# Gated window attention on one core: pairing each small query tile with part of a late one, and moving four kinds of work between steps and engines

## The chip, the cores and the metric

The kernel runs on one core of a Trainium2 chip. The metric is the device time of one execution in microseconds, given as the median of several runs. Everything is computed in float32 (one product is done in a float32 split into two passes, some small constants are bfloat16).

## The reference

Eight sequences of 1024 tokens with 512 features go through a layer norm, a masked attention with 16 heads of 32 features, and a gate computed from the same normalised input. Cut to what matters:

```python
xn = _layernorm(x)                       # x: (8, 1024, 512)
q, k, v = proj(Wq, bq), proj(Wk, bk), proj(Wv, bv)      # 16 heads, dk = 32
scores = einsum('bhid,bhjd->bhij', q, k) / sqrt(dk)
im = arange(L) % 256                     # four windows of 256 tokens
scores = where(im[:, None] >= im[None, :], scores, -1e30)
attn = einsum('bhij,bhjd->bhid', softmax(scores), v)
s = attn.reshape(B, L, D) @ Wo.T + bo
w = (weights >= 0) * 2 - 1
g = silu(clip((xn @ w.T) * scale + bias, -100, 100))
out = x + s * g
```

A token sees the tokens of all four windows whose place in their window is not later than its own. The kernel orders tokens by place first and window second, so that the mask becomes a causal one: in eight tiles of 128 tokens, query tile i sees key tiles 0 to i.

## The kernel before

**Groups and steps.** Four heads fill the 128 partitions, so a sequence has four head groups; a pair (b, g) is called a group, and there are 32. Every group takes nine steps, n = 0 to 8, in the main loop (L1257). A step holds attention work for the present group and, at the same time, for the next one (`nxt`), and it is filled up with projections, gate products and output products (`fill`, L1267).

**The quad.** Four PSUM banks form one tile, a *quad* (`quad`, L535), with 512 columns for each of four heads. There is one quad only, so every use waits until the readers of the use before have finished. A group uses it 16 times:

- Nine S quads (`maxima_quad`, L547) hold scores with queries on the partitions. `S_QUADS` says which query tile and which keys are in each. For the late query tiles 4 to 7, VectorE takes the maximum over the keys (L585, tile `pm`). For the early query tiles 0 to 3 VectorE takes the negated maximum (L579, `nm`), and ScalarE takes the exponentials straight from the quad (`own_probs`, L604, `pd`).
- Seven T quads (`probs_quad`, L747, in all steps but 0 and 3) hold the scores of late queries once more, with keys on the partitions and the maxima subtracted; ScalarE takes the exponentials of a quad in one instruction (L786, `p`). `attend_quad` (L792) multiplies them with the values one step later, and GpSimd adds them up for the row sums (`add_probs`, L814).

**Early tiles.** Their exponentials have to be turned, so that keys come onto the partitions. `own_turn` (L653) transposes blocks of 32x32 on VectorE (L658) into the tile `pt`, and 16 DMAs of one block each (`move`, L664), issued by SyncE, put the blocks into the tile `px`. There is one buffer for `pt` and one for `px`. `own_sums` (L614) makes the row sums on VectorE, and `own_attend` (L676) multiplies `px` with the values on TensorE. The moves are kept in a list, and every call of `fill` issues four of them. The tiles `pd` and `p` share two buffers.

`DIRECT` lists the S quads with early tiles and how many blocks of 128 keys these have: quad 0 (tile 3), quad 3 (tiles 2 and 0), quad 6 (tile 1, beside a part of tile 5). The turn and the sums of quads 0, 3 and 6 are done at the start of steps 1, 4 and 7, and the products of the turned blocks come three steps later: in steps 4 and 7, and in step 1 of the group after.

**Filling work.** Two further PSUM banks (`bank`, L123) take the products that fill the steps. Such a product (`product`, L383) has four chunks with a planned cost of 0.86 each; after the last one the bank is emptied: values, queries and keys by ScalarE (L421, L438), gate and output products by VectorE (two instructions each, L470 and L471, L866 and L867). A product can't start in a bank that has not been emptied. The order of filling work in each group is written in `STEADY`, `OPENING` and `CLOSING` (L932): V values, q, k queries and keys, G and H gate products, O and P output products, N the next sequence's layer norm; what stands before "|" may be taken a group early. How much of it goes into a step is planned by `share`: an even part of the remaining cost, less a fixed number for each step (L1153), with a least amount after an S quad (L1329) and a wanted amount between a T quad and its S quad (`gap`, L1309).

**Other steps' work.** In step 0 ScalarE copies the attention result of the group before (`copy_heads`) and its row sums (`sum_keys`, L832). VectorE inverts those sums in four parts, two in step 3 and two in step 5 (`invert`, L836), and applies them in step 6 (L840).

Each engine runs its instructions in the order in which they are written.

Of the kernel before, what the change touches and what calls it, by code (L numbers as in the profile page):

```python
# [46 lines left out]
    [(2, 0, 384), (0, 0, 128)],  # L47
    [(4, 0, 512)],
    [(5, 0, 512)],
    [(1, 0, 256), (5, 512, 768)],  # L50
    [(7, 512, 1024)],
    [(6, 512, 896), (4, 512, 640)],
# [17 lines left out]
DIRECT = {0: 4, 3: 4, 6: 2}  # L70

@with_exitstack
def tile_gated_window_attention(
# [307 lines left out]
    vt, qt, kt, gd = {}, {}, {}, {}  # L381

# [34 lines left out]
    def values_work(b, it):  # L417
        def after(ps):

            vt[b, it] = vpool.tile([P, D], F32, tag="v", name=f"v_{b}_{it}")  # L420
            nc.scalar.copy(vt[b, it], ps)  # L421
# [9 lines left out]
    def heads_work(b, g, half, which):  # L431
# [3 lines left out]
        def after(ps):  # L435
            if (b, g) not in into:
                into[b, g] = qk.tile([P, L], F32, tag=which, name=f"{which}_{b}_{g}")
            nc.scalar.activation(  # L438
                into[b, g][:, half * HALF : (half + 1) * HALF], ps, AF.Identity,
                bias=bias[:, g : g + 1], scale=SCALE if which == "q" else 1.0,  # L440
            )
# [172 lines left out]
    def own_sums(b, g, n):  # L614
        it = direct[b, g, n]
        if n == 0:
# [3 lines left out]
        for i, lo, hi, at in it["own"]:  # L620
            part = view[:, :, :, at // P : (at + hi - lo) // P]
            nc.vector.tensor_reduce(  # L622
                inverse[b, g][:, i, :], part.rearrange("p h r k t -> p h r (k t)"), AX.XY, ALU.add
            )
        if n == 6:
            nc.vector.reciprocal(inverse[b, g], inverse[b, g])
# [26 lines left out]
    def own_turn(b, g, n):  # L653
        it = direct[b, g, n]
        size = NH * DIRECT[n] * P
        t = swapped.tile([P, NH * HALF], F32, tag="pt", name=f"pt_{b}_{g}_{n}")
# [4 lines left out]
        def move(q, r):  # L661
            if "x" not in it:
                it["x"] = swapped.tile([P, NH * HALF], F32, tag="px", name=f"px_{b}_{g}_{n}")
# [4 lines left out]

        moves.extend(lambda q=q, r=r: move(q, r) for r in range(NH) for q in range(NH))
# [6 lines left out]
    def own_attend(b, g, n):  # L676
        it = direct.pop((b, g, n))
        k = DIRECT[n]
# [18 lines left out]
        if n == 6:  # L697
            copy_heads(b, g, 0)

    def copy_heads(b, g, f):  # L700
        aT[b, g, f] = heads.tile([P, HALF], F32, tag=f"a{f}", name=f"aT_{b}_{g}_{f}")
        nc.scalar.copy(aT[b, g, f], av[b, g, f])
# [117 lines left out]
    def sum_keys(b, g):  # L820
# [11 lines left out]
        nc.scalar.copy(sums[b, g], ps)  # L832
# [75 lines left out]
    def row_work():  # L908
# [24 lines left out]
        "V4 G3 V5 q20 | V7 G4 V6 k20 q21 G5 k21",  # L933
        "O0 O1 O2 | q30 N0 k30 O3 q31 G6 k31 G7",
        "N1 O4 O5 | O6 k00' V0' q00' O7 V1' q01'",
        "V2' V3' | k01' q11' G0' k10' G1' k11' q10' G2'",
# [4 lines left out]
        "N1 G6 G7 V1' V2' k00' q00' V3' q01'",  # L941
        "k01' G0' | q11' k10' R G1' k11' q10' G2'",
# [4 lines left out]
        "H3 O4 H4 O5 H5 O6 H6 O7 |",  # L947
# [203 lines left out]
    def side(b, g):  # L1151
        if (b, g) not in sides:
            sides[b, g] = Beside(beside(b, g), [1.8, 1.43, 2.7, 0.86, 1.86, 1.86, 1.36, 2.3, 1.86])  # L1153
# [78 lines left out]
    start += values_work(0, 0) + values_work(0, 1) + values_work(0, 2) + values_work(0, 3)  # L1232
    start += heads_work(0, 0, 1, "k")
    start += woven(heads_work(0, 1, 0, "k"), fw_turns[:2])
# [3 lines left out]
    for n in range(NQ):  # L1238
        if n in (1, 4, 7):
            own_turn(0, 0, n - 1)  # L1240
            own_sums(0, 0, n - 1)
        maxima_quad(0, 0, n)
        if n == NQ - 1:
# [5 lines left out]
        if n in (5, 8):  # L1249
            own_attend(0, 0, n - 5)  # L1250
        if n not in (4, 7):
            move_some(9)
        start.fill(share)
    start.fill(1e9)

    steps = [(b, g, n) for b in range(B) for g in range(NC) for n in range(NQ)]
    for s, (b, g, n) in enumerate(steps):  # L1257
# [20 lines left out]
        if nxt and n in (1, 4, 7):  # L1278
            own_turn(*nxt, n - 1)
            own_sums(*nxt, n - 1)  # L1280
        spent = 0.0
        if n in (0, 3):
# [4 lines left out]
            if before:  # L1287
                attend_quad(*before)
            if nxt:
                own_probs(*nxt, n)  # L1290
            if n == 0 and old:
                copy_heads(*old, 1)
                spent += fill(1.2, turns=0)
                sum_keys(*old)
                spread_inverse(b, g)
            elif n == 0:
                spread_inverse(b, g)
        else:
# [3 lines left out]
            if n == 1:  # L1302
                own_attend(b, g, 6)
# [119 lines left out]
```

## Time and profile before

| what | value |
|---|---|
| median of 3 runs | 2381.21 us (2376.27 to 2389.77) |
| the profiled execution, its own time | 2391.47 us |
| its span, first to last instruction | 2389.7 us |
| TensorE (PE) busy | 2131.2 us, 89% |
| VectorE (DVE) busy | 1516.1 us, 63% |
| GpSimd (POOL) busy | 1141.7 us, 48% |
| ScalarE (ACT) busy | 946.0 us, 40% |
| mean granted TensorE clock | 0.969 |
| DMA, 16 engines | 28.9% busy on the queue that SyncE issues to |

Busy time counts every instruction of an engine from its start to its end, overlaps once. A matmul's end is modelled, so PE's busy time is not PE at its peak. The waits list names, for each engine and line, the idle time before an instruction and the instruction whose semaphore ended it. In the profile an fp32 matmul shows as two instructions. "PE t L753" is the first matmul of a T quad, "PE s L555" and "PE s L565" are the first of an S quad.

### The profile page before, as it was taken

What the parts mean: (1) busy time and instruction counts of PE and PEld (TensorE: products, weight loads), DVE (VectorE), ACT (ScalarE), POOL (GpSimd) and SP (SyncE); (2) the same over time, 40 slices, a digit from 0 to 9 for tenths busy, and PEclk for the clock granted to TensorE, in tenths of its full rate; (3) what the DMA queues carried; (4) which work ended last, traced back from release to release, by engine and by line L of the source; (5) the groups of instructions that cost most, each with busy time, mean ns of one, the idle gap of its engine ahead of it and who ended that gap; (6) DMA issues with size and microseconds to landing.
All of it is one profiled execution on the core that took longest, in us unless ns stands there. A gap on an engine that the chain in (4) does not pass through costs nothing. (4 is left out here: it accounts for less than half of the span.)

```text
span 2389.7 us, 59945 instructions
## 1 busy us (share of the span) xinstructions
PE 2131.2 (89%) x25775; PEld 897.8 (38%) x25775; DVE 1516.1 (63%) x1667; ACT 946.0 (40%) x1312; POOL 1141.7 (48%) x1037
## 2 busy tenths in 40 slices
PE   8899899999989898998989989898889888899877
PEld 4334333333333333333334333333333333333332
DVE  4657666766666656676566765667656667576763
ACT  3245444444443343344433343434434344443331
POOL 1056454554635445363454544555445555445556
PEclk9999999999999999999999999999999999999989
DMA  6222223332223322243212332223312233223233
GB/s 199 62 61 73 68 52 82 98 114 55 69 72 102 102 60 53 72 115 94 68 50 78 105 98 63 59 78 100 107 50 74 78 101 100 51 59 89 81 89 103
DMA packets 136610, 196.12 MB, mean 82 GB/s; under 512 B 31116, under 2 KB 51864, under 8 KB 136344
## 3 DMA queue, kind: packets, MB, share of 16 engines
q1 hardware_dynamic: 135640, 191.10, 28.9%
q8 instruction: 203, 3.33, 0.6%
q10 hardware_dynamic: 704, 1.18, 0.1%
q14 instruction: 63, 0.52, 0.1%
HBM read 72.62 MB, written 35.65 MB: 45 GB/s over the span
## 5 line engine op out<-in xcount | busy, mean ns | idle before, releaser
L814 POOL TENSOR_TENSOR p<-p,p 128x512 f32<-128x512 f32 (+1 forms) x736 | 890.6, 1241 | 484.9 <-ACT p L786 481.9
L585 DVE TENSOR_REDUCE pm<-s 128x4 f32<-128x2048 f32 (+3 forms) x256 | 480.2, 1886 | 345.3 <-PE s L565 343.9
L786 ACT ACTIVATE p<-t 128x2048 f32<-128x2048 f32 (+1 forms) x224 | 393.7, 1758 | 562.6 <-PE t L763 279.2
L604 ACT ACTIVATE pd<-s,nm 128x384 f32<-128x384 f32 (+3 forms) x512 | 224.4, 535 | 353.7 <-DVE nm L579 232.3
L565 PE MATMUL s<-k,q 32*128 32x512 f32 (+3 forms) x3072 | 318.4, 507 | 15.0 <-ACT p L786 10.5
L395 PE MATMUL v_ps<-wvT,xnT 128*32 128x512 f32 (+3 forms) x2792 | 254.2, 489 | 16.6 <-ACT sums L832 10.2
L395 PE MATMUL k_ps<-xnT,wk 128*32 128x512 f32 (+3 forms) x2632 | 254.5, 505 | 3.3 <-ACT sums L832 2.0
L579 DVE TENSOR_REDUCE nm<-s 128x2 f32<-128x1024 f32 (+3 forms) x256 | 195.8, 817 | 91.5 <-PE s L565 90.8
L395 PE MATMUL q_ps<-xnT,wq 128*32 128x512 f32 (+3 forms) x2672 | 247.9, 488 | 6.3 <-ACT xnT L366 4.1
L395 PE MATMUL o_ps<-woT,aT 128*32 128x512 f32 (+3 forms) x2624 | 244.4, 497 | 8.6 <-DVE s L867 6.9
L658 DVE STREAM_TRANSPOSE pt<-pd 128x2048 f32<-128x2048 f32 (+1 forms) x96 | 187.5, 1953 | 86.1 <-ACT pd L604 68.7
L763 PE MATMUL t<-q,k 32*128 32x512 f32 (+3 forms) x2048 | 232.5, 536 | 0.0
L799 PE MATMUL av<-p,v 128*32 128x512 f32 (+3 forms) x2048 | 230.2, 534 | 0.1
L868 POOL TENSOR_TENSOR s<-s,xb 128x512 f32<-128x512 f32 x63 | 84.4, 1340 | 220.1 <-DVE s L867 188.0
L472 POOL TENSOR_SCALAR y<-y 128x512 f32<-128x512 f32 x64 | 41.9, 655 | 308.0 <-DVE y L471 245.3
L622 DVE TENSOR_REDUCE ls<-pd 128x4 f32<-128x2048 f32 (+3 forms) x128 | 183.2, 1451 | 0.0
L493 PE MATMUL y_ps<-fwT,x 128*128 128x512 f32 x472 | 148.7, 451 | 35.5 <-ACT q L438 14.9
L565 PEld LDWEIGHTS s<-k,q 32*128 32x128 f32 x3072 | 129.3, 185 | 101.4 <-ACT p L786 72.2
L753 PE MATMUL t<-shift,neg 3*128 3x512 bf16 (+3 forms) x1024 | 88.8, 356 | 74.7 <-ACT pd L604 38.9
L395 PEld LDWEIGHTS v_ps<-wvT,xnT 128*32 128x32 f32 x2792 | 84.3, 111 | 167.4 <-issue 128.1
L466 POOL TENSOR_TENSOR x<-xnT,x 128x512 fp32r<-128x512 f32 x59 | 75.9, 1286 | 143.2 <-ACT x L465 141.8
L395 PEld LDWEIGHTS o_ps<-woT,aT 128*32 128x32 f32 x2624 | 81.9, 110 | 159.5 <-issue 139.9
(111 smaller groups left out, 1938.4 us busy)
## 6 DMA issues: line engine op xcount, KB each, us to landing
px<-pt SPq DMA_DIRECT2D x1024, 64.0 KB, 2.0
px<-pt SPq DMA_DIRECT2D x512, 32.0 KB, 1.9
g<-t SPq DMA_DIRECT2D x64, 256.0 KB, 2.0
gb<-g SPq DMA_DIRECT2D x64, 256.0 KB, 3.1
xb<-in_L_attn_x_dram SPq DMA_DIRECT2D x64, 256.0 KB, 3.3
out_dram<-s SPq DMA_DIRECT2D x63, 256.0 KB, 2.5
x<-in_L_attn_x_dram SPq DMA_DIRECT2D x62, 256.0 KB, 3.5
wk<-wk_d SPq DMA_DIRECT2D x31, 256.0 KB, 3.3
```

The lines of the kernel that those rows point to most:

```text
L395: nc.tensor.matmul(hold[0][cols, lo:hi], lhsT=lhsT[:, cols], rhs=rhs[:, lo:hi], start=(i == 0 and lo == 0), stop=(i == n - 1), skip_group_ ...
L493: nc.tensor.matmul(hold[0], lhsT=part[i][:, c, :], rhs=wT["fw"][:, c, :], start=(i == 0 and c == 0), stop=(i == 1 and c == NC - 1),)
L565: nc.tensor.matmul(sc[:, h, at : at + hi - lo], lhsT=qt[b, g][head_rows(h), i * P : (i + 1) * P], rhs=kt[b, g][head_rows(h), lo:hi], start ...
L579: nc.vector.tensor_reduce(nm[:, k, h : h + 2], sc[:, h : h + 2, at : at + hi - lo], AX.X, ALU.max, negate=True,)
L585: nc.vector.tensor_reduce(pm[:, 0 if lo == 0 else 1, i - 4, :], sc[:, :, at : at + hi - lo], AX.X, ALU.max,)
L604: nc.scalar.activation(view[:, h, at // P : (at + hi - lo) // P], it["sc"][:, h, at : at + hi - lo].rearrange("p (k r t) -> p k r t", r=NH ...
L622: nc.vector.tensor_reduce(inverse[b, g][:, i, :], part.rearrange("p h r k t -> p h r (k t)"), AX.XY, ALU.add)
L658: nc.vector.transpose(t[:, 0:size], it["p"][:, 0:size])
L763: nc.tensor.matmul(sc[:, h, at : at + w], lhsT=kt[b, g][head_rows(h), j * P : (j + 1) * P], rhs=qt[b, g][head_rows(h), HALF + lo : HALF + ...
L786: nc.scalar.activation(pt[:, :, :width], sc[:, :, :width], AF.Exp, scale=1.0)
L799: nc.tensor.matmul(av[b, g, 1][head_rows(h), lo : lo + w], lhsT=vt[b, j][:, g * P + h * DK : g * P + (h + 1) * DK], rhs=pts[b, g, n][:, h, ...
L814: nc.gpsimd.tensor_tensor(t[:, hs, lo : lo + w], t[:, hs, lo : lo + w], p[:, hs, at : at + w], ALU.add)
```

## The change

The S quads are put together anew. Tile 2 (384 keys) shares quad 3 with 128 keys of tile 4; tile 1 (256 keys) moves from quad 6 to quad 5, with the same part of tile 5; tile 0 (128 keys) moves from quad 3 to quad 7, with 384 keys of tile 6; quad 8 is now a part of tile 7 alone. All quads keep 512 columns. `DIRECT` now has four quads: 0, 3, 5 and 7, with 4, 3, 2 and 1 blocks of 128 keys, in place of 4, 4 and 2.

There are thus four turns a group, each with 16 moves. Those of quads 0, 5 and 7 stand at the start of steps 1, 6 and 8; that of quad 3 stands within step 3, after some filling work. The sums of quad 0 are split: two heads before, two heads after the S quad of step 1. The products of the turned blocks stand in step 3 (quad 0), 6 (quad 3), 8 (quad 5) and in step 1 of the group after (quad 7). The turned tile of quad 7 lies in a buffer of the pool for temporaries in place of `pt`.

In step 0, VectorE empties the banks of values, queries and keys; it also makes the copy of the attention result and the copy of the row sums, which ScalarE made before. The four inversions stand in steps 2, 4, 6 and 7, and are applied in step 8. One gate product and one key projection change places between the lists of the groups, and the planned amounts of filling work are new. The first group's order is adapted (not shown).

```diff
-    [(2, 0, 384), (0, 0, 128)],
+    [(2, 0, 384), (4, 512, 640)],
     [(4, 0, 512)],
+    [(1, 0, 256), (5, 512, 768)],
     [(5, 0, 512)],
-    [(1, 0, 256), (5, 512, 768)],
+    [(0, 0, 128), (6, 512, 896)],
     [(7, 512, 1024)],
-    [(6, 512, 896), (4, 512, 640)],
...
-DIRECT = {0: 4, 3: 4, 6: 2}
+DIRECT = {0: 4, 3: 3, 5: 2, 7: 1}
...
-            nc.scalar.copy(vt[b, it], ps)
+            if by_vector[0]:
+                nc.vector.tensor_copy(vt[b, it], ps)
+            else:
+                nc.scalar.copy(vt[b, it], ps)
...
+            if by_vector[0]:
+                nc.vector.tensor_scalar(dst, ps, factor, bias[:, g : g + 1], ALU.mult, ALU.add)
...
+        small_one = n == 7 and b < B - 1
+        if small_one:
+            t = temp(f"pt_{b}_{g}_{n}")
...
+        while it["left"]:
+            move_some(1)
...
-        nc.scalar.copy(sums[b, g], ps)
+        nc.vector.tensor_copy(sums[b, g], ps)
...
-        "V4 G3 V5 q20 | V7 G4 V6 k20 q21 G5 k21",
+        "V4 V5 q20 | V7 G4 V6 k20 q21 G5 k21",
         "O0 O1 O2 | q30 N0 k30 O3 q31 G6 k31 G7",
-        "N1 O4 O5 | O6 k00' V0' q00' O7 V1' q01'",
-        "V2' V3' | k01' q11' G0' k10' G1' k11' q10' G2'",
+        "N1 O4 O5 | O6 k00' V0' q00' O7 V1' q01' k01'",
+        "V2' V3' | q11' G0' k10' G1' k11' q10' G2' G3'",
...
-            sides[b, g] = Beside(beside(b, g), [1.8, 1.43, 2.7, 0.86, 1.86, 1.86, 1.36, 2.3, 1.86])
+            sides[b, g] = Beside(beside(b, g), [1.9, 1.17, 2.7, 1.72, 0.95, 1.81, 2.0, 1.4, 2.2])
...
-        if nxt and n in (1, 4, 7):
-            own_turn(*nxt, n - 1)
-            own_sums(*nxt, n - 1)
+        if nxt and n in (1, 6, 8):
+            done = {1: 0, 6: 5, 8: 7}[n]
+            own_turn(*nxt, done)
+            own_sums(*nxt, done, slice(0, 2) if n == 1 else slice(0, NH))
         spent = 0.0
+        by_vector[0] = n == 0
...
+            if n == 3 and nxt:
+                own_attend(*nxt, 0)
...
             if n == 1:
-                own_attend(b, g, 6)
+                own_attend(b, g, 7)
...
-            elif n in (4, 7) and nxt:
-                own_attend(*nxt, n - 4)
+            elif n in (6, 8) and nxt:
+                own_attend(*nxt, n - 3)
             if nxt:
-                gap = {1: 1.6, 2: 0.4, 4: 1.2, 6: 0.2, 7: 0.8}.get(n, 1.2)
+                gap = {1: 2.0, 2: 0.5, 4: 2.2, 6: 0.2, 7: 1.8, 8: 1.0}.get(n, 1.4)
...
+                if n == 1:
+                    own_sums(*nxt, 0, slice(2, NH))
...
-        if old and n in (3, 5):
-            invert(*old, n - 3)
-            invert(*old, n - 2)
-        if old and n == 6:
+        if old and n in (2, 4, 6, 7):
+            invert(*old, {2: 0, 4: 1, 6: 2, 7: 3}[n])
+        if old and n == 8:
             normalise_heads(*old)
...
-            want = max(want, 2.45 if len(S_QUADS[n]) > 1 else 2.35)
+            want = max(want, {5: 2.9, 7: 2.8}.get(n, 2.35))
...
-            fill(max(want, (2.4 if n == 0 else 4.4) - spent) if nxt else want)
+            if n == 3 and nxt:
+                want -= fill(1.6)
+                own_turn(*nxt, 3)
+                own_sums(*nxt, 3)
+            fill(max(want, 2.4 - spent) if nxt else want)
```

## The prediction

> **What bounds the kernel now.** I read the page first, then one windows answer for each step number, then PE's waits, and last the timeline of one group.
>
> ```profile
> span 2389.7 us, 59945 instructions
> ...
> PE 2131.2 (89%) x25775; PEld 897.8 (38%) x25775; DVE 1516.1 (63%) x1667; ACT 946.0 (40%) x1312; POOL 1141.7 (48%) x1037
> ```
>
> TensorE (PE) is the bound, with 258.5 us idle. The change leaves its instructions alone: nine S quads of 512 columns, 40 blocks of turned products and the same filling work. So the time can only move with PE's idle time. The windows run from a step's first quad matmul to the next step's, for steps 0 to 8 in this order; each sum is over 27 groups, the second to the 28th.
>
> ```profile
> sum 232.15, PE 186.97 PEld 63.38 DVE 177.24 ACT 123.53 POOL 93.93; mean PE 6.92 PEld 2.35 DVE 6.56 ACT 4.58 POOL 3.48
> sum 219.18, PE 196.56 PEld 73.72 DVE 171.79 ACT 83.20 POOL 35.92; mean PE 7.28 PEld 2.73 DVE 6.36 ACT 3.08 POOL 1.33
> sum 204.95, PE 202.22 PEld 82.15 DVE 94.94 ACT 80.03 POOL 106.28; mean PE 7.49 PEld 3.04 DVE 3.52 ACT 2.96 POOL 3.94
> sum 235.13, PE 195.22 PEld 89.09 DVE 135.26 ACT 100.61 POOL 71.05; mean PE 7.23 PEld 3.30 DVE 5.01 ACT 3.73 POOL 2.63
> sum 213.30, PE 196.37 PEld 82.63 DVE 191.31 ACT 104.01 POOL 132.67; mean PE 7.27 PEld 3.06 DVE 7.09 ACT 3.85 POOL 4.91
> sum 193.85, PE 193.40 PEld 67.27 DVE 87.83 ACT 68.05 POOL 132.25; mean PE 7.16 PEld 2.49 DVE 3.25 ACT 2.52 POOL 4.90
> sum 210.21, PE 176.10 PEld 81.02 DVE 158.17 ACT 86.30 POOL 126.03; mean PE 6.52 PEld 3.00 DVE 5.86 ACT 3.20 POOL 4.67
> sum 247.51, PE 217.01 PEld 114.38 DVE 150.31 ACT 90.23 POOL 116.73; mean PE 8.04 PEld 4.24 DVE 5.57 ACT 3.34 POOL 4.32
> sum 198.80, PE 197.45 PEld 88.03 DVE 98.20 ACT 69.19 POOL 147.14; mean PE 7.31 PEld 3.26 DVE 3.64 ACT 2.56 POOL 5.45
> ```
>
> Sum less PE, over 27, is the idle time a group: 1.67, 0.84, 0.10, 1.48, 0.63, 0.02, 1.26, 1.13 and 0.05 us in steps 0 to 8, 7.18 in all, of 72.4. PE's waits say on what:
>
> ```profile
> PE t L753 <- ACT pd L604: 38.9, 33, 4.2
> PE s L555 <- ACT p L786: 33.9, 31, 2.8
> PE t L753 <- DVE pm L585: 32.8, 22, 3.9
> PE y_ps L493 <- ACT q L438: 14.9, 8, 2.9
> PE y_ps L493 <- ACT v L421: 13.7, 5, 2.7
> ...
> PE v_ps L395 <- ACT sums L832: 10.2, 5, 2.0
> ```
>
> The first three are the quad: about once a group in step 6 (pd), step 7 (p), steps 1 and 4 (pm). The others are banks not yet emptied, in steps 3 and 0. The timeline shows step 6 and the queue of SyncE (SP):
>
> ```profile
> 1209.96 7.47 SPq L664 DMA_DIRECT2D px<-pt  x12
> ...
> 1224.29 0.33 SPq L482 DMA_DIRECT2D g<-t  x1
> 1224.66 12.37 SPq L664 DMA_DIRECT2D px<-pt  x12
> 1224.98 1.29 DVE L579 TENSOR_REDUCE nm<-s 128x2 f32<-128x512 f32 x2 [0.72 <-PE s L565]
> 1226.19 1.21 DVE L585 TENSOR_REDUCE pm<-s 128x4 f32<-128x1024 f32 x1
> 1227.52 1.57 ACT L604 ACTIVATE pd<-s,nm 128x256 f32<-128x256 f32 x4 [3.87 <-DVE pm L585]
> 1229.13 0.40 PE L753 MATMUL t<-shift,neg 3*128 3x384 bf16 x8 [1.51 <-ACT pd L604]
> ```
>
> In a quad shared by an early and a late tile, ScalarE starts pd only after pm, though it needs only nm. A move takes 0.63 us of SP (7.47 / 12), and one g write held the moves behind it by some 6.8 us.
>
> **The change, step by step.** Idle us a group, before to after.
>
> *Step 6 to steps 5 and 7.* Quad 6 becomes plain, so step 6's wait for pd goes. Quad 5 gets the old quad 6's readers: its S quad begins at 1223.75, the next T quad 5.38 later; the quad itself takes 1.16, and PE filled 2.7 for a planned 2.45. Now 2.9 is planned, some 3.2 us: wait 1.0. Quad 7 reads 2 x 0.413 (nm) + 1.755 (pm, the row of 1536) + pd, 4 x 0.385 less the overlap of the 256 row (1.57 of 1.90): 3.85 in place of 4.07. With 2.8 planned: wait 0.9. Both could be 0.4 to 1.5.
>
> *Step 7's wait for p.* Here p takes the buffer that pd left, so it waits for the turn and sums (ACT p waited 66.0 us for L622). That pair is now in steps 6 and 8. Step 6: turn 1.24, sums 1.18, then p of 256 columns, 1.03: 3.5 after pd, while PE has T quad 0.8, products 1.06 + 0.80 (12 of 16 blocks' 1.06) and 0.2: wait 0.65. Step 8: turn about 0.7 (rows 2.31 and 1.24 halved on), sums 0.67, no longer than the T quad's own 1.4: nothing new, 0.05. Step 7: no such wait left beyond the 0.9.
>
> *Steps 1 and 4, pm behind turn and sums.* In step 1 1.12 of the 2.24 sums goes behind pm. In step 4, turn and sums were 2.31 + 1.71 + 0.67 = 4.69; now they begin within step 3 and take about 1.75 + 1.71 = 3.46, and PE needs pm only some 4.8 after the T quad starts. 0.63 to 0.2. In step 1 VectorE also has step 0's new copies ahead of it, so I take 0.84 to only 0.5 (0.1 to 1.5).
>
> *Step 3's banks.* Bank copies stand on ScalarE behind pd: eight instructions, 4 x 0.594 + 4 x 0.385 = 3.92, now four, 2.38; nm and pm are 2.58 against 2.73. Banks come free 1.7 sooner, about the wait itself: 1.48 to 0.4 (0 to 1.5).
>
> *Step 0.* The result copy (0.59) and sums copy (0.62) stood on ScalarE behind nm (2.43) and pd (2.42); on VectorE they wait for nm alone. That ends the waits on ACT sums. But the waits there on DVE s and y (o_ps, v_ps, sum, mT: about 28 us in all) stay, and the result copy is put ahead of those empties. With 0.34 less filling planned: 1.67 to 1.0 (0.3 to 1.7). VectorE takes 0.69 for a bank (rows L470, L866) where ScalarE takes 0.59 to 0.62: two copies, and at 3.4 of filling against 3.44 a product, with three products in four of them V, q or k, under one bank: about 1.9 us a group. The Trainium skill ("VectorE: DVE Perf Modes", Specifications) says VectorE sits closer to SBUF and ScalarE closer to PSUM, which speaks against this move. The rows agree in sign, by 0.1 us an instruction; going by distance alone the step would lose 0.3 us instead of gaining, and I go by the queue, since 4.85 us of queue stood ahead on ScalarE.
>
> *Inversions* (4 x 0.92) move behind pm, into steps 2, 6 and 7, whose VectorE is 3.5 to 5.9 busy of 7.6 to 9.2 us, and step 4, which loses turn work: nothing. Step 8's apply (0.84) stands where 3.64 was busy: nothing; were it before pm, 0.84. Quad 7's turned tile holds one of five temporary buffers for some 13 us; all waits for such a buffer now are 2.5 us (ACT t on a write to out_dram), so nothing, and up to 0.7 where gate and output banks had to wait for one. The gate product that leaves group 0 takes with it 8.4 of the 28 us of step 0 at most; this is within that step's 1.0.
>
> The sum: 1.0, 0.5, 0.1, 0.4, 0.2, 1.0, 0.65, 0.9, 0.05 = 4.8; gain 2.38.
>
> *SP and px.* Moves go from 48 to 64 a group, 10.1 us more of SP; smaller blocks issue no faster (32 KB and 64 KB both about 0.59). px has one buffer. For quad 7 it comes free 3.0 into step 8 and is needed 1.46 into step 1: 7.36 - 3.0 + 7.6 + 1.46 = 13.4 us. Sixteen moves take 10.1, landing 2.0, two other issues 1.2: 13.3. No slack, where before there were three steps and PE waited for px once (2.6 us). Held moves as shown would take 17.1 + 2.0 = 19.1: wait 5.7. SP's own waits list has 106 such holds (g 51, out_dram 55; 443 us), 0.37 a step, 4.2 us each. Over the 1.5 steps in which moves remain that is 0.55 a group, each costing about 2 after what SP can catch up: 1.1. Quad 0, with 1.6 of slack, and the others I take at zero. Bounds 0 to 4.
>
> Net 2.38 - 1.1 = 1.28 a group, 35 us over 27 groups; the opening and the other five groups I leave even (10 either way). Against the profiled execution, 2391.47 (span 2389.7 and 1.8 outside), that is 2357; it stands 10.3 above the median, so the median becomes 2347.
>
> **Rivals.** No wait for px (SP runs ahead, holds fall elsewhere): 2.38 x 31 = 74, so 2307; with steps 0 and 3 at their low ends 2280. For: before, one wait in 31 groups. Against: the slack is gone.
>
> No change: VectorE is full in steps 0 and 1. It is busy 12.9 of 16.7 there; with 1.9 more it has 14.8 of about 15.1, in order, and each late pm holds the next T quad. If step 1 idles at 1.6 and step 0 keeps 1.2, the net is zero: 2380. For: DVE's st waits up to 4.8 us for a load of x. Against: VectorE waits for pd in step 0 anyway, so the copies fit there.
>
> Slower: the px chain. If moves are held in most groups, PE waits at the turned products of step 1 (and 3); a mean of 3.4 us a group costs 1.0 net, 31 us: 2412. It decides from 2.4 us a group on. For: 19.1 against 13.4. Against: holds come in a third of the steps.
>
> That VectorE empties next to nothing in step 0 is possible too; the two copies are the part that counts.
>
> **How the numbers follow.** The forecast (2318 to 2369) 0.44, no px wait 0.20, VectorE full 0.17, px chain 0.19. About 0.5%, 12 us, is what a measurement of this kernel can tell from no change. Faster 0.64, same 0.17, slower 0.19. The range 2293 to 2405 leaves out the low part of the second case and the high half of the last. The forecast's own range is 2318 to 2369.
>
> **What would show it.** Right: no "t <- pd" in step 6 but two in steps 5 and 7, near 1 us each; "s <- p" in step 6 at half its size; "v_ps <- ACT sums" gone; "av <- px" some 30 us. Wrong: idle in steps 0 and 1 of 2.5 or more together; "av <- px" under 5 or over 75 us; PE busy other than 2131 by over 15.

## The result and the profile after

The changed kernel takes 2456.72 us (median of 4 runs, 2454.36 to 2462.35), the kernel before 2381.93 beside it: a ratio of 1.0315, 95% interval 1.028 to 1.035. It is slower by 75 us. The forecast was 2347, and the time lies above the whole range. Of the rivals the px chain came nearest, with 2412.

First the page of the changed kernel, its span and TensorE's busy time.

```profile
span 2452.6 us, 60762 instructions
...
PE 2145.0 (87%) x25655; PEld 895.5 (37%) x25655; DVE 1574.2 (64%) x1802; ACT 911.0 (37%) x1241; POOL 1139.7 (46%) x1038
```

The profiled execution took 2454.36. Its span is 62.9 us longer than the one of before: 13.8 of it is TensorE's busy time (2145.0 against 2131.2, though the profile has 120 matmuls fewer), 49 its idle time (307.6 against 258.5).

Now the windows, cut as before at the first matmul of each step's quad, steps 0 to 8 in this order, sums over the 27 groups from the second to the 28th.

```profile
sum 199.57, PE 186.90 PEld 63.58 DVE 167.53 ACT 91.26 POOL 74.32; mean PE 6.92 PEld 2.35 DVE 6.20 ACT 3.38 POOL 2.75
sum 207.31, PE 198.65 PEld 73.61 DVE 164.52 ACT 97.75 POOL 29.00; mean PE 7.36 PEld 2.73 DVE 6.09 ACT 3.62 POOL 1.07
sum 205.80, PE 201.04 PEld 84.92 DVE 127.08 ACT 79.72 POOL 102.39; mean PE 7.45 PEld 3.15 DVE 4.71 ACT 2.95 POOL 3.79
sum 200.87, PE 200.02 PEld 103.42 DVE 141.12 ACT 89.97 POOL 61.12; mean PE 7.41 PEld 3.83 DVE 5.23 ACT 3.33 POOL 2.26
sum 209.01, PE 199.00 PEld 74.60 DVE 144.16 ACT 86.21 POOL 120.16; mean PE 7.37 PEld 2.76 DVE 5.34 ACT 3.19 POOL 4.45
sum 251.61, PE 216.28 PEld 98.53 DVE 149.90 ACT 115.06 POOL 189.31; mean PE 8.01 PEld 3.65 DVE 5.55 ACT 4.26 POOL 7.01
sum 208.24, PE 181.39 PEld 74.36 DVE 154.00 ACT 49.20 POOL 89.21; mean PE 6.72 PEld 2.75 DVE 5.70 ACT 1.82 POOL 3.30
sum 233.43, PE 204.94 PEld 89.69 DVE 139.46 ACT 91.33 POOL 121.51; mean PE 7.59 PEld 3.32 DVE 5.17 ACT 3.38 POOL 4.50
sum 265.98, PE 175.50 PEld 74.56 DVE 129.81 ACT 76.92 POOL 175.59; mean PE 6.50 PEld 2.76 DVE 4.81 ACT 2.85 POOL 6.50
```

Sum less PE, over 27, beside the prediction's numbers, in us a group:

| step | 0 | 1 | 2 | 3 | 4 | 5 | 6 | 7 | 8 | all |
|---|---|---|---|---|---|---|---|---|---|---|
| before | 1.67 | 0.84 | 0.10 | 1.48 | 0.63 | 0.02 | 1.26 | 1.13 | 0.05 | 7.18 |
| predicted, without px | 1.0 | 0.5 | 0.1 | 0.4 | 0.2 | 1.0 | 0.65 | 0.9 | 0.05 | 4.8 |
| after | 0.47 | 0.32 | 0.18 | 0.03 | 0.37 | 1.31 | 0.99 | 1.06 | 3.35 | 8.08 |

Steps 0 to 7 come to 4.73 where 4.75 was predicted. That the sums agree so well is partly luck: steps 0 to 3 idle 1.0 us less than predicted, steps 4 to 7 about 1.0 more. What made the kernel slower within these groups stands in step 8. PE's waits name it:

```profile
PE av L709 <- DMA px<-pt: 71.5, 25, 5.5
PE t L776 <- ACT pd L612: 70.3, 64, 4.2
PE s L563 <- DVE pm L593: 44.3, 29, 2.6
```

In the profile before, the first and the third of these were small (the second was 38.9):

```profile
PE s L555 <- DVE pm L585: 6.8, 9, 2.7
...
PE av L686 <- DMA px<-pt: 2.6, 1, 2.6
```

In step 8 of the 27 groups the first row has 47.8 us in 12 waits and the third 37.3 in 20: 85.1 of the 90.5 us of idle time there. The rows of single groups in the windows answer for step 8 (columns: length, then busy time of PE and its matmuls, of the other engines, granted clock, DMA) show which groups; these are the four of the second sequence:

```profile
456.39:469.86 13.47, 6.14 (x69) 2.72 (x68) 5.21 (x7) 1.88 (x1) 10.57 (x13) 0.87 0.23 70
534.73:541.76 7.03, 4.45 (x68) 2.12 (x68) 5.12 (x7) 2.35 (x2) 4.29 (x4) 1.00 0.42 131
604.99:612.43 7.44, 7.41 (x100) 2.97 (x100) 3.83 (x5) 3.50 (x4) 5.29 (x5) 1.00 0.08 17
674.56:687.45 12.89, 8.88 (x101) 3.27 (x100) 5.06 (x7) 3.34 (x4) 7.03 (x7) 0.87 0.41 124
```

Two causes are visible. The first and second groups have 68 matmuls (the same step of before had 85 to 113): the quads and the attention products, and as filling only eight matmuls of one output product. And the first and fourth groups are 5 to 6 us longer than the others, at a lower clock. The timeline of a first group shows why (steps 6 to 8, SyncE's queue, its releasers on GpSimd and what waits):

```profile
1323.29 4.96 SPq L684 DMA_DIRECT2D px<-pt  x8
...
1331.86 0.64 SPq L892 DMA_DIRECT2D out_dram<-s  x1
1332.60 0.54 SPq L490 DMA_DIRECT2D g<-t  x1
...
1334.47 2.45 SPq L684 DMA_DIRECT2D px<-pt  x4
1336.73 1.27 POOL L891 TENSOR_TENSOR s<-s,xb 128x512 f32<-128x512 f32 x1 [4.89 <-DMA xb<-in_L_attn_x_dram]
1338.02 0.64 SPq L892 DMA_DIRECT2D out_dram<-s  x1
...
1339.40 8.20 SPq L684 DMA_DIRECT2D px<-pt  x8
1343.48 0.64 PE L709 MATMUL av<-px,v 128*32 128x128 f32 x16 [4.34 <-DMA px<-pt]
...
1349.49 0.24 PE L563 MATMUL s<-after,place_of 32*128 32x128 bf16 x4 [2.42 <-DVE pm L593]
```

Quad 5's sixteen moves go out as 8, 4 and 4 (the row x8 at 1339.40 begins with the last four; quad 7's follow). After the first eight the queue stands 3.6 us, until 1331.86, before a write to out_dram. The last four stand behind a second such write, which waits for GpSimd's `s`, which waits for a load of xb. They are issued from 1339.40 on; four times some 0.62 and a landing of 2.0 give 1343.9, and PE's products begin at 1343.48. Then the next S quad waits 2.42 us for pm, with nothing to fill in.

### The profile page after: what moved, and what is told of

Read it like the earlier page. It is cut to its first block, busy times and chain, and to the rows that moved or that the text cites. A ratio compares the mean times of both kernels' runs of the same rounds, so it can differ in the third digit from the quotient of the medians.

```text
span 2452.6 us, 60762 instructions
## 1 busy us (share of the span) xinstructions
PE 2145.0 (87%) x25655; PEld 895.5 (37%) x25655; DVE 1574.2 (64%) x1802; ACT 911.0 (37%) x1241; POOL 1139.7 (46%) x1038
## 3 DMA queue, kind: packets, MB, share of 16 engines
q10 hardware_dynamic: 704, 1.18, 0.1%
## 5 line engine op out<-in xcount | busy, mean ns | idle before, releaser
L612 ACT ACTIVATE pd<-s,nm 128x256 f32<-128x256 f32 (+3 forms) x512 | 228.3, 529 | 490.2 <-DVE pm L593 387.8
L573 PE MATMUL s<-k,q 32*128 32x512 f32 (+3 forms) x3072 | 344.7, 542 | 43.0 <-ACT p L809 41.6
L671 DVE STREAM_TRANSPOSE pt<-pd 128x2048 f32<-128x2048 f32 (+3 forms) x128 | 193.2, 1510 | 118.1 <-ACT pd L612 86.3
L396 PE MATMUL o_ps<-woT,aT 128*32 128x512 f32 (+3 forms) x2664 | 253.5, 503 | 9.8 <-DVE y L479 9.5
L396 PE MATMUL q_ps<-xnT,wq 128*32 128x512 f32 (+2 forms) x2728 | 253.0, 490 | 0.9 <-DVE sign L280 0.8
L396 PE MATMUL k_ps<-xnT,wk 128*32 128x192 f32 (+3 forms) x2520 | 240.7, 506 | 0.8
L822 PE MATMUL av<-p,v 128*32 128x512 f32 (+3 forms) x2048 | 241.1, 557 | 0.0
L630 DVE TENSOR_REDUCE ls<-pd 128x2 f32<-128x1024 f32 (+4 forms) x159 | 189.1, 1190 | 0.0
L709 PE MATMUL av<-px,v 128*32 128x128 f32 x2560 | 100.9, 287 | 76.6 <-DMA px<-pt 71.5
L776 PE MATMUL t<-shift,neg 3*128 3x512 bf16 (+3 forms) x1024 | 86.0, 344 | 83.7 <-ACT pd L612 70.3
L396 PEld LDWEIGHTS q_ps<-xnT,wq 128*32 128x32 f32 x2728 | 82.8, 112 | 167.1 <-issue 145.2
```

The costliest lines, as they stand in the source:

```text
L396: nc.tensor.matmul(hold[0][cols, lo:hi], lhsT=lhsT[:, cols], rhs=rhs[:, lo:hi], start=(i == 0 and lo == 0), stop=(i == n - 1), skip_group_ ...
L573: nc.tensor.matmul(sc[:, h, at : at + hi - lo], lhsT=qt[b, g][head_rows(h), i * P : (i + 1) * P], rhs=kt[b, g][head_rows(h), lo:hi], start ...
L612: nc.scalar.activation(view[:, h, at // P : (at + hi - lo) // P], it["sc"][:, h, at : at + hi - lo].rearrange("p (k r t) -> p k r t", r=NH ...
L630: nc.vector.tensor_reduce(inverse[b, g][:, i, hs], part[:, hs].rearrange("p h r k t -> p h r (k t)"), AX.XY, ALU.add,)
L671: nc.vector.transpose(t[:, 0:size], it["p"][:, 0:size])
L709: nc.tensor.matmul(av[b, g, 0][head_rows(h), i * P : (i + 1) * P].rearrange("p (q t) -> p q t", t=MT), lhsT=vt[b, j][:, g * P + h * DK : g ...
```

## The experiments

Ratios are to the kernel before, run on the same chip in between, with the 95% interval; waits in us are PE's, from each kernel's own profile. In the expectations, theory 1 is that late moves in SyncE's queue cost the time, theory 2 that the filling runs out before step 8, theory 3 that VectorE is too full, and theory 4 that the two waits for pd a group cost it.

### The moves

Eight moves at each call of `fill`, in the changed kernel:

```diff
-            move_some(4)
+            move_some(8)
```

> The changed kernel, but every filling call issues eight moves in place of four, so that a turned tile's 16 moves stand in SyncE's queue ahead of the writes to out_dram that hold it. If the px chain on SyncE is what costs (theory 1): PE's waits for px fall from 71.5 us to under 20, the half-clock stretches after them go too, and the median falls by 60 to 100 us, to 2357 to 2397. If the planned filling that runs out before step 8 is what costs (theory 2): the waits for px fall as well, but PE then waits in step 8 for p and pm, and the median falls by less than 30 us, to above 2427.

2426.12 us, 1.018 [1.0157, 1.0202]: 31 less, between what the two theories said. The wait for px is 10.4 in place of 71.5, and it is gone from step 8; waits on pd (75.0) and of S quads on pm (47.8) stay.

```profile
PE av L709 <- DMA px<-pt: 10.4, 5, 5.5
```
The same stretch of its timeline has all sixteen moves of quad 5 ahead of the first held write:

```profile
1308.11 11.14 SPq L684 DMA_DIRECT2D px<-pt  x16
1319.35 0.64 SPq L892 DMA_DIRECT2D out_dram<-s  x1
```

The order in SyncE's queue is thus enough to make px late or not. Other things come later instead: VectorE now waits 59.4 us for rows of x (15 times; 7.3 in the changed kernel), whose loads stand behind the moves, and a smaller row of the changed kernel, o_ps on VectorE's y in step 5, grows from 9.5 to 28.7. What the late rows of x cost by themselves is not shown; the version with both repairs below still has 53.7 us of that wait.

All sixteen at once:

```diff
-            move_some(4)
+            move_some(16)
```

> The changed kernel with all 16 moves of a turn issued in the first filling call. If the time of the px chain is only a matter of order in SyncE's queue: waits for px fall below the 10 us of moves8 and the median to 2405 to 2425. If sixteen moves in one go hold other transfers (gate and token reads, output writes): the waits move to o_ps and y_ps and the median is at or above that of moves8, 2426 to 2450.

2464.68 us, 1.0337 [1.0307, 1.0366]. Px is at 12.4, but VectorE waits 91.1 us for rows of x and PE 109.3 for pd. More moves ahead no longer help px. The loads of x come later still, and pd too; whether the one makes the other late was not followed up.

The fourth part of the issues for the same bytes, each turned tile in four transfers. This version leaves out that a block is brought to its own partitions, so its output is not that of the reference, and it serves for its time alone:

```diff
-                it["x"][r * MT : (r + 1) * MT, q * block : (q + 1) * block],
-                t[q * MT : (q + 1) * MT, r * block : (r + 1) * block],
+                it["x"][:, q * block : (q + 1) * block],
+                t[:, q * block : (q + 1) * block],
...
-        it["left"] = NH * NH
-        moves.extend(lambda q=q, r=r: move(q, r) for r in range(NH) for q in range(NH))
+        it["left"] = NH
+        moves.extend(lambda q=q: move(q, 0) for q in range(NH))
...
-            move_some(4)
+            move_some(1)
```

> The changed kernel, with each turned tile moved by 4 transfers over all 128 partitions in place of 16 block transfers: the same bytes, a quarter of the issues on SyncE's queue, one issued at each fill point. Left out: a block is not brought to its own partitions, it stays where the turn put it. Theory 1 (the number of issues on SyncE is what makes px late): TensorE's waits for px fall from 71.5 us to under 10, VectorE's waits for rows of x stay under 15 us since the queue is never long, and the time falls by 35 to 55 us, to 2400 to 2422; what stays above the kernel before is the empty step 8 (s after pm, still 40 to 50 us) and the two waits for pd. Theory 2 (px is late for another reason: the copy out of the bank, or the landing itself): px still waits 50 us or more and the time stays above 2440.

2410.38 us, 1.0129 [1.0099, 1.0159]: 46 less than the changed kernel, within theory 1's times. But the wait for px is 40.2, between what the two theories said. What is left, 35.5 us of it in step 8, is the other half of the same cause:

```profile
1303.39 0.58 SPq L892 DMA_DIRECT2D out_dram<-s  x1
1304.07 0.56 SPq L883 DMA_DIRECT2D xb<-in_L_attn_x_dram  x1
1304.69 4.01 SPq L684 DMA_DIRECT2D px<-pt  x2
1307.53 0.65 PE L709 MATMUL av<-px,v 128*32 128x128 f32 x16 [3.00 <-DMA px<-pt]
```

The fourth transfer still goes out behind the held write. So fewer issues take off 31 us of wait, and the position in the queue accounts for the rest, as far as this group shows it; theory 1 as written, by the number alone, was too simple. The time fell by more than the wait: idle time by 32 us, PE's busy time by 18 (2127.0 against 2145.0). That second part goes with the clock, see the end.

The writes to out_dram issued by GpSimd instead of SyncE:

```diff
-            nc.sync.dma_start(tokens(out, b, it), s)
+            nc.gpsimd.dma_start(tokens(out, b, it), s)
```

> The changed kernel with the writes to out_dram of the output products issued by GpSimd, behind its own addition, in place of SyncE, so that SyncE's queue is not held by them. Theory 1 (moves are late because SyncE stands before out_dram): the waits for px fall from 71.5 to under 25 us and the median by 20 to 35 us, as with moves8. If the moves are late because there are 64 of them at 0.63 us: the waits for px stay above 50 us. [...]

2466.3 us, 1.0365 [1.034, 1.039], no faster than the changed kernel. Px falls to 43.4, so the held writes do count, but the wait for pd rises to 96.6, and nothing is gained by having GpSimd issue them (0.58 us of its time for each, in the median). Why pd came later was not followed up.

The reverse in the kernel before: products of quads 0 and 3 one step earlier, filling shifted with them, so that 16 moves have two steps in place of three.

```diff
-            elif n in (4, 7) and nxt:
-                own_attend(*nxt, n - 4)
+            if n == 3 and nxt:
+                own_attend(*nxt, 0)
...
+            elif n == 6 and nxt:
+                own_attend(*nxt, 3)
```

> The kernel before with the turned products of quads 0 and 3 one step earlier (steps 3 and 6 in place of 4 and 7), the filling of those steps shifted by the same amount, and the rest as it was: the moves get two steps in place of three. Theory 1 in its sharper form (what costs is the shorter time for the same moves, not their number): PE's waits for px rise from 2.6 to 20 to 60 us and the median by 15 to 50 us, to 2397 to 2432. If two steps are enough for 16 moves at 48 a group: waits for px under 10 us and 2370 to 2390.

2397.96 us, 1.0071 [1.0047, 1.0094]. The wait for px goes from 2.6 to 33.6 us (26 times), in a kernel with 48 moves a group and no shared quads of the new kind. Two steps are thus often too short for sixteen moves issued four at a call. The median is 17 us above that of the kernel before. The profile can't account for this rise, since its execution, 2388.59, was the fastest of six; in it waits for p and pm are lower (s on p 29.2 in place of 44.4, t on pm 21.6 in place of 32.8).

### The filling

The kernel before with higher least amounts in steps 4, 5 and 7, so that its list runs short in step 8:

```diff
-            want = max(want, 2.45 if len(S_QUADS[n]) > 1 else 2.35)
+            want = max(want, {4: 3.4, 5: 3.1, 7: 3.6}.get(n, 2.45 if len(S_QUADS[n]) > 1 else 2.35))
```

> The kernel before with only its least amounts of filling after the S quads of steps 4, 5 and 7 raised (3.4, 3.1, 3.6), so that step 8 is left with 1.9, 0, 2.3 and 3.1 of planned cost in groups 0 to 3 in place of 3.6, 4.0, 3.9 and 3.5, and with none in parts of the first and the last sequence, as in the changed kernel. Theory 2: PE's wait of an S quad for pm, 9 us before, rises to 30 to 50 us, steps 4, 5 and 7 grow, and the median rises by 25 to 50 us, to 2409 to 2434. If running out of filling costs nothing by itself: 2375 to 2395.

2431.5 us, 1.021 [1.0186, 1.0235], with nothing else changed. The row that the profile after has in step 8 appears here, twice as large:

```profile
PE s L555 <- DVE pm L585: 84.3, 26, 8.0
```

It was 6.8 in the kernel before, and 75.9 of the 84.3 lie in step 8 of the 27 groups. An empty step is therefore a loss by itself; it needs neither the new quads nor VectorE's copies.

The changed kernel with amounts set so that step 8 keeps some:

```diff
+        share = {0: 2.6, 3: 2.9}.get(n, 0.0) if (b, g) < (B - 1, 2) else share
...
-                gap = {1: 2.0, 2: 0.5, 4: 2.2, 6: 0.2, 7: 1.8, 8: 1.0}.get(n, 1.4)
+                gap = {1: 1.5, 2: 0.3, 4: 2.1, 6: 0.9, 7: 1.7, 8: 0.6}.get(n, 1.1)
...
-            want = max(want, {5: 2.9, 7: 2.8}.get(n, 2.35))
+            want = max(want, {5: 3.3, 7: 3.2}.get(n, 2.35))
...
-            fill(max(want, 2.4 - spent) if nxt else want)
+            fill(max(want, 2.4 - spent if n == 0 else 0.8) if nxt else want)
```

> The changed kernel with other amounts of planned filling and nothing else: less between T and S quads in steps 1, 2, 4, 5, 7 and 8, less in step 3, more after the S quads of steps 5 and 7 and in step 6, so that step 8 gets 2.6, 1.4, 2.9 and 2.8 of planned cost in groups 0 to 3 where the changed kernel leaves it 0.5, 0.5, 3.4 and 2.6. Theory 2 (the filling runs out before step 8): PE's wait of the S quad of step 0 for pm falls from 46 to under 20 us, that for pd from 70 to about 50, and the median falls by 30 to 50 us, to 2405 to 2425. Theory 1 alone (the px chain): the waits for px stay at 70 us and the median falls by less than 15.

2500.17 us, 1.0496 [1.0479, 1.0513]: the waits of S quads on pm fall from 45.7 to 17.6, as meant, and px rises to 88.7. The time is 43 us above the changed kernel. Of the wait for px 58.9 us now lie in step 1, at the products of quad 7, and 20.4 in step 8. With px in the way the filling moved does not help.

Both together, that filling and `move_some(8)`:

> The planned filling of plan_only and eight moves a filling call as in moves8. If theories 1 and 2 are both right and add up: waits for px under 15 us, for pm in the S quad of step 0 under 20 us, and a median of 2365 to 2395, level with the kernel before or a little under it. If the pairing of the tiles itself costs (theory 4: two waits for pd a group in place of one): PE still waits 60 us or more for pd and the median stays above 2400.

2392.37 us, 1.0041 [1.0026, 1.0055], 64 below the changed kernel, where the two edits alone gave -31 and +43. Step 8 idles 0.96 us a group in place of 3.35; steps 0 and 3 idle 1.54 and 0.62 in place of 0.47 and 0.03. Px is at 17.5, S quads on pm at 15.6 in both their lines, pd at 65.7.

```profile
PE t L776 <- ACT pd L612: 65.7, 71, 4.2
...
PE av L709 <- DMA px<-pt: 17.5, 11, 5.5
...
PE s L563 <- DVE pm L593: 14.2, 16, 2.4
```

The two repairs together thus take back all of the loss but 10 us; and the two causes hide each other. This does not make the new quads nearly free, though. Eight moves a call and VectorE in step 0 are a gain in the kernel before too (2361.43 us with both, at the end of the experiments), and beside that version this one is 31 us slower. Its profile has 65.7 us of waits for pd in place of 39.3 there and 17.5 for px in place of 2.1, against 9.7 of T quads for pm in place of 32.4.

The changed kernel with the lists of filling work of before:

```diff
-        "V4 V5 q20 | V7 G4 V6 k20 q21 G5 k21",
+        "V4 G3 V5 q20 | V7 G4 V6 k20 q21 G5 k21",
...
-        "N1 O4 O5 | O6 k00' V0' q00' O7 V1' q01' k01'",
-        "V2' V3' | q11' G0' k10' G1' k11' q10' G2' G3'",
+        "N1 O4 O5 | O6 k00' V0' q00' O7 V1' q01'",
+        "V2' V3' | k01' q11' G0' k10' G1' k11' q10' G2'",
```

(and the opening and closing lists likewise).

> The changed kernel with the lists of filling work (STEADY, OPENING, CLOSING) of the kernel before: the gate product G3 back in group 0, the key projection k01 back in group 3, H3 back in the last sequence. Theory 2 (group 0 and 1 run out of work before step 8): PE's wait of the S quad of step 0 for pm falls from 44.3 to under 15 us, the output products are no longer drawn into group 0 and with them goes half of the wait for px; median 2390 to 2420. Theory 1 alone: the wait for px stays at 60 us or more and the median above 2430.

2435.15 us, 1.0219 [1.0194, 1.0245]: 22 less. Px is at 54.6 and S on pm at 37.4. The new lists made both waits somewhat worse.

### VectorE in step 0

The changed kernel with ScalarE emptying the banks of step 0 again:

```diff
-        by_vector[0] = n == 0
+        by_vector[0] = False
...
-        nc.vector.tensor_copy(sums[b, g], ps)
+        nc.scalar.copy(sums[b, g], ps)
...
-                    copy_heads(*old, 1, nc.vector.tensor_copy)
+                    copy_heads(*old, 1, nc.scalar.copy)
```

> The changed kernel with ScalarE doing in step 0 what it did before: it empties the banks of values, queries and keys and makes the copies of the attention result and of the row sums. If VectorE in step 0 was a gain, as the fall of step 0 from 8.60 to 7.39 us suggests: step 0 goes back to 8.3 to 8.6, and the median rises by 20 to 35 us, to 2477 to 2492. If the copies on VectorE cost something elsewhere (a late turn, a late pm in step 1, theory 3): the median falls or stays, 2440 to 2460.

2459.91 us, 1.0321 [1.0295, 1.0346]: the same as the changed kernel. Step 0 idles 0.57 us a group in it, against 0.47 in the changed kernel and 1.67 in the kernel before, so the fall of step 0 is not VectorE's doing. VectorE empties only eight banks of values, queries and keys in the whole changed kernel; its part is in the main the two copies. The reverse, the kernel before with VectorE in step 0 (the result and sums copies likewise):

```diff
+            if by_vector[0]:
+                nc.vector.tensor_copy(vt[b, it], ps)
+            else:
+                nc.scalar.copy(vt[b, it], ps)
...
+        by_vector[0] = n == 0
```

> The kernel before with this one part of the change: in step 0 VectorE empties the banks of values, queries and keys and makes the two copies. Part pays by itself: step 0's idle time falls from 1.67 to 0.5 to 1.0 us a group and the median by 15 to 35 us, to 2347 to 2367. Theory 3 (VectorE is full in steps 0 and 1, the wait moves to the T quad of step 2): 2375 to 2395.

2377.24 us, 0.9974 [0.996, 0.9987], some 6 us faster: step 0 idles 1.20 in place of 1.67, but step 1 1.18 in place of 0.84. And ScalarE in step 0 of the version with both repairs, the edit of `scalar_step0` on that version:

> plan_moves8 (2392) with ScalarE in step 0 as before, now that px waits no longer stand over it. If VectorE's part pays as it does in the kernel before (6 us there): 2394 to 2410. If it does nothing or costs in this kernel: 2380 to 2394.

2421.46 us, 1.0158 [1.013, 1.0185], 29 slower than that version; a wait on ScalarE's v of 23.1 us appears. So this part of the change is a gain, of a size that depends on what else is late: nothing, 6 or 29 us.

### The two waits for pd

The version with both repairs, with the maxima (pm) of shared quads taken in two halves, so that pd might start after the first:

```diff
+                for h in range(0, NH, 2 if own else NH):
+                    hs = slice(h, h + (2 if own else NH))
-                nc.vector.tensor_reduce(
-                    pm[:, 0 if lo == 0 else 1, i - 4, :], sc[:, :, at : at + hi - lo],
+                    nc.vector.tensor_reduce(
+                        pm[:, 0 if lo == 0 else 1, i - 4, hs], sc[:, hs, at : at + hi - lo],
```

> plan_moves8 with the pm of the shared quads (3, 5, 7) taken in two halves, two heads each, so that ScalarE can take the exponentials of the first two heads while VectorE reads the other two banks. Theory 4 (what is left over is the two waits for pd a group): the readers of quads 5 and 7 end 0.5 to 0.8 us sooner, PE's wait for pd falls from 66 to 20 to 35 us, and the median falls by 25 to 45 us, to 2347 to 2367. If pd waits for all of pm whatever its parts, or the wait is not on the path: no change, 2385 to 2400.

2392.33 us, 1.0043 [1.0029, 1.0058]: nothing. The timeline shows it; two halves as one row, then pd:

```profile
1312.12 1.81 DVE L595 TENSOR_REDUCE pm<-s 128x2 f32<-128x768 f32 x2
1314.05 1.14 ACT L614 ACTIVATE pd<-s,nm 128x128 f32<-128x128 f32 x4 [3.99 <-DVE pm L595]
```

pd starts 0.12 us after the end of the second half; in all 96 shared quads it is 0.08 to 0.39 us. The same edit in the kernel before with VectorE in step 0:

> before_vector0 (2377) with the same halving of pm, here in quad 6 alone. If pd behind pm is on the path: PE's wait for pd falls from 35 to about 15 us, the median by 10 to 20 us, to 2357 to 2367, under both kernels. If not: 2372 to 2382.

2380.21 us, 0.9985 [0.9967, 1.0003]: nothing either.

### The first group, and versions under both

The version with both repairs, sixteen moves a call, and the first group's quad 5 products in step 1 instead of step 0:

```diff
+                if s == 1:
+                    own_attend(b, g, 5)
...
-        if s == 0:
-            own_attend(b, g, 5)
```

> plan_moves8 with 16 moves a call, and in the first group the turned products of quad 5 one step later, in step 1. If the first group's 10 us over the kernel before are its wait for px (5.5 us, and the half clock after it): the first group falls from 79 to 69 to 73 us and the median by 6 to 12 us, to 2380 to 2386, level with the kernel before. If not: 2390 to 2400.

2447.75 us, 1.0269 [1.024, 1.0298]. Two things were changed at once: with sixteen a call VectorE's wait for rows of x is 77.0 us in place of 53.7, and PE's wait of o_ps for ScalarE's xnT 42.9 in place of 20.3. So the run says nothing on the first group. The version with both repairs, with the edits of `split_pm` and `old_lists` and `move_some(16)` for the opening's `move_some(9)`:

> split_pm with the lists of the kernel before and with all 16 moves of a turn issued at once in the opening. The first group's wait for px (8 us there in plan_moves8) goes and the last sequence has its gate product back: 5 to 15 us under split_pm. If lists and opening don't matter: equal to split_pm within 5 us.

2430.19 us, 1.0199 [1.0174, 1.0224], worse by 38 than without these edits: bank waits of before are back (y_ps on ScalarE's v 18.2, q 17.4 us; 3.0 and 1.3 without). That points to the lists, which would then suit only the filling amounts they are used with; but the opening was changed at once, and the two were not separated.

The kernel before with more moves at a call:

```diff
-            move_some(4)
+            move_some(8)
```

> A control: the kernel before with eight moves a filling call. It waited for px once (2.6 us), so there is nothing to gain: 2372 to 2392. If eight moves a call help by something else than the waits for px: below 2365.

2367.81 us, 0.9929 [0.9904, 0.9954]: faster, where nothing was expected. The wait for px was one of 2.6 us and is one of 2.1, so the gain has another source; see the clock at the end. With VectorE in step 0 as well:

> The kernel before, with eight moves issued at a fill point in place of four, and VectorE in place of ScalarE for the bank-emptying of step 0. If the two gains are independent (13 us and 6 us below the kernel before, each alone) they add: 2360 to 2364. If both take away the same idle time, 2366 to 2371; if the earlier moves hold up rows of x that VectorE, now with more to do, needs sooner, 2372 or more.

2361.43 us, 0.9914 [0.9895, 0.9933]: inside 2360 to 2364, so the two gains add. It is the fastest version found, 0.9% under the kernel before, and its quads are those of the kernel before. In its profile px is one wait of 2.1 us, and step 0 idles 1.19 us a group in place of 1.67.

## Why the prediction was wrong

**Px: right cause, wrong place, wrong size.** The step that failed is "Quad 0, with 1.6 of slack, and the others I take at zero". The sum was made for quad 7, needed in step 1; there the wait is 6.1 us in 27 groups. It stands at quad 5, needed in step 8: 47.8 us. Quad 5 has two steps, as quad 7 has, but in the group shown above two writes to out_dram and one to g lie in the queue between its first and its last move, not the 0.55 holds a group of an even spread. All of px is 2.0 us a group in place of 1.1. The stated test ("wrong if over 75 us") let 71.5 pass; it was too wide, since removing only part of that wait gave 46 us.

**Step 8 empty: not in the sum.** The prediction put the raised amounts of steps 5 and 7 in as cover and costed "Step 8 [...] nothing new, 0.05". It never asked which step pays for the filling. The same lists feed nine steps; 68 matmuls in step 8 of two groups in four are what was left. The wait on pm there is 37.3 / 27 = 1.4 us a group. That such emptiness costs time is shown in the kernel before (+2.1%); that it and px together make up most of the loss is shown by the version with both repairs, 64 us faster with 0.96 us of idle time a group in step 8.

**Outside the 27 groups: "I leave even".** The first group took 80.0 us in place of 69.5 (px waits of 5.5 and 4.1 there), the 29th to 31st 236.9 in place of 205.7: together 42 of the span's 62.9; the opening and the last group gave back 5.5. In those three groups PE's idle time goes from 25.6 to 47.3 us: pd +10.5, px +8.0, p +5.6, pm +2.6. `moves8` has 220.1 there, the version with both repairs 215.4. The first group is a matter of px too: it still takes 79 in those two versions, with px waits of 8.5 and 8.4 us, and 68.1 in `four_moves`, with none.

**What was right.** Two waits for pd near 1 us: 70.3 us in 64 waits, 0.85 a group in each of steps 5 and 7 for 1.0 and 0.9 (with smaller waits, for y and p, these steps idle 1.31 and 1.06). The bank waits of steps 0 and 3 went: v_ps on ScalarE's sums is no longer listed, step 3 is at 0.03. Steps 0 and 1 idle 0.79 together, far from 2.5, so VectorE was not full there. The Trainium skill ("VectorE: DVE Perf Modes", Specifications) has ScalarE closer to PSUM, which spoke against VectorE's copies. That agrees with the time of one copy (0.59 to 0.62 us on ScalarE, 0.69 on VectorE) but did not decide the kernel's: no run with ScalarE in step 0 was faster than its partner with VectorE.

**Right by luck.** Step 0 was to gain by VectorE's copies, 1.67 to 1.0. It fell to 0.47, but `scalar_step0`, without VectorE there, has 0.57. What did change is the filling: in the 27 groups step 0 holds 240 matmuls of output products in place of 512. `before_starved`, the old kernel with an empty step 8, has the same 240 and idles 0.90 in step 0, 0.05 in step 1 and 0.80 in step 3, all lower than before. So a part of what steps 0 to 3 gained is the other side of the empty step 8, and with step 8 filled again it is smaller (1.54, 0.52, 0.12 and 0.62). In the kernel before, VectorE's copies moved part of the idle time from step 0 to step 1, as the rival of a full VectorE had it.

**Mis-sized:** the wait for p in step 6, 0.65 predicted, is 25.8 / 27 = 0.96. Halving turn and sums did not halve it.

**The balance.** 27 groups were to gain 35 us and lost 26.7: 2.0 - 1.1 of px and 1.4 of filling make 2.3 a group, or 62. The first group and the 29th to 31st lost 42 where none was put down, and the opening and the last group gave back 5.5. The px rival was to decide from 2.4 us a group on; px alone came to 2.0 in the 27 groups, so it took the empty step to make the kernel slower by so much.

So steps 0 to 7 did idle 2.4 us a group less, as predicted: 3.35 less in steps 0 to 4, while steps 5 to 7, with the newly paired quads, rose from 2.41 to 3.36. But with step 8 filled again, in the version with both repairs, they idle 5.87 in place of 7.13, which is 1.3 less. The 16 further moves and the filling moved to cover the new pd waits cost more. With both repaired, the kernel is still 31 us behind the old quads with eight moves a call and VectorE in step 0; which part of the change keeps it there is not separated.

## What to carry to other kernels

When a change raises the filling of some steps, write down the whole list against all steps and see which comes last: that step pays. When it adds transfers to an in-order queue, look for the transfer with the most held writes between its first and last part, not for the one with the shortest time on average; and try issuing them earlier before moving work, since that alone was worth 0.7% in the old kernel. Test two suspected causes together as well as apart: here one repair looked harmful until the other was made. And give the old kernel the same repairs before you judge the change by what they gain: here it gained from them too.

## What was not expected of the hardware

**Idle time that comes together costs more than the same idle time spread out.** In the profiles the granted clock changes in stretches of 3.41 us or multiples of it. Counting idle time of PE in the stretch before: with 1.8 us or more of it, the stretch that follows ran at half the clock in 35 of 38 cases before and in 47 of 48 after; with less than 0.5 us in none of 538 and none of 515; between, in 9 of 121 and 20 of 152. A 128x512 matmul of the filling took 1.06 us in these stretches and 0.59 outside them. Time at half clock went from 150.9 us to 229.8. In the 27 groups 115.9 of it lies in step 8 and the step 0 that follows (62.7 and 53.2), where the profile before has 13.8, all in step 0. PE's busy time within these stretches is 137 us before, 183 after and 147 in `four_moves`; if all its matmuls are slower by 1.06 to 0.59, an estimate, that adds 20 us from before to after and takes 16 off again in `four_moves`, where PE's busy time grew by 13.8 and fell by 18. The gain of eight moves in the kernel before is of this kind too: half clock 150.9 to 103.0 us, busy time 2131.2 to 2111.9, idle time 258.5 to 254.3 only (the profiled execution of before stood 10 us above its median, so part of that difference is its own). The Trainium skill ("TensorE: Matmul & The Clock Gate", Why this matters for your kernels) warns of idle gaps of more than about 3 us. Here 1.8 us in all within a stretch were enough in nearly all cases.

**The issue of a move costs the same whatever its size.** SyncE took 0.59 us (median) for a move of 32 to 64 KB in the kernel before and 0.60 for one of 64 to 256 KB in `four_moves`; the largest landed 1.1 us later (3.1 in place of 2.0). Other transfers differ: a write of g, 256 KB, took 0.33. Where the queue is the limit, the number of transfers counts.

**pd waits for all of pm.** With pm written in two halves into one tile, ScalarE's pd, which reads neither, began only after the second, in all 96 shared quads of that profile. Whether the order of the instructions or the shared banks of the quad make it wait was not separated.
